# State-space stage: decay from sums broadcast by DMA, block output made transposed

## The chip, the cores and the metric

The kernel runs on one core of a Trainium2 chip. The metric is the time of one execution on the device, in microseconds (us). The engines are named as in the profile: PE is TensorE's matmul, PEld its weight load, DVE is VectorE, ACT is ScalarE, POOL is GpSimd, SP is SyncE, which here only issues DMAs.

## The reference, cut to what matters

The program is a two-layer decoder over 16 sequences of 128 tokens and width 256. Each layer has an attention-like part, a cross attention and a feed-forward part; the change lies in the attention-like part of the second layer, a state-space block with 8 heads of width 64, a state of 128 and chunks of 64. In the reference it reads (cut):

```python
xn = _rmsnorm(x, norm_w)
zxbcdt = xn @ in_proj_w                      # z: 512, xBC: 768, dt: 8
dt = jax.nn.softplus(zxbcdt[..., -NHEADS:] + dt_bias)
conv = conv_b + sum((xpad[:, k:k + T, :] * conv_w[:, k] for k in range(D_CONV)))
xBC = jax.nn.silu(conv)                      # xs: 512, Bm: 128, Cm: 128
y = _ssd(xs * dt[..., None], dt * A, Bm, Cm) # y_t = sum over s <= t of (C_t . B_s) exp(cs_t - cs_s) dt_s xs_s
y = y + xs * D[None, None, :, None]
y = _rmsnorm(y * jax.nn.silu(z), ssm_norm_w)
y = y @ out_proj_w
```

Here `cs` is the running sum of `dt * A` along the tokens, per head. The result `y` is then scored, the best tokens are gathered into a memory of 50 slots, and attention over that memory follows. A sequence has 128 tokens, so the kernel computes the whole recurrence of a sequence as one lower triangular 128x128 product per head.

## The kernel before, in words

A token block is one sequence: 128 tokens on the 128 partitions, 16 blocks in all. `K.x[b]` holds the residual of block b in SBUF during the whole kernel. The stages follow each other: mixture of experts (stage 0), cross attention and feed-forward of layer 0 (stage 1), the state-space block and its memory (stage 3), cross attention of layer 1 (stage 4), mixture of experts of layer 1 (stage 5). Everything is in float32 in the stage at hand.

The functions of `ssm` do the following. `normed(g)` normalizes a group of four blocks and turns it, so that `xnT[g]` has features on partitions and 512 tokens along the row. `convolved(g, c)` makes 128 channels of the convolution for the 512 tokens of group g: two products, one ACT operation, three DVE taps, a Tanh, and a finishing DVE operation (L1296); the result `cT[g]` is transposed too, channels on partitions. `steps()` makes `dt` and `da = dt * A` for all blocks at once, tokens on partitions.

Then for each block n. `decay(n)` makes the decay matrix `mT` of the 8 heads, source token on partitions and target token along the row: POOL writes `run`, the upper triangle times `da`; two products with the strictly lower triangle turn it into differences of running sums (`ps_seg`); ACT takes the exponential. `inner(n)` makes the product of B and C (`ps_s`), masks it on DVE (`bc`), and POOL multiplies `mT` by it; PE turns the four 128-channel pieces of `cT` (`px`), and DVE makes `xd` (times `dt`) and `yr` (times `D`) from them. `gate(n)` makes z with tokens on partitions, and its SiLU (`sz`). `outer(n)` multiplies, for each head, `mT` by `xd` into `py`, with tokens on partitions; DVE adds `yr`, POOL multiplies by `sz`, ACT squares with a sum along the row, POOL makes the reciprocal root `yrs`. `turned(n)` transposes the gated value by four PE transposes and an ACT copy, `projected(n)` applies the output projection, ACT scales by `yrs`, and DVE adds to the residual. `kept(n)` turns the result into `m.yT`; `remembered(g)`, `ranked(g)` and `counted(g)` do scores and ranks for each group of four blocks.

The order of work is set in two ways. PE's instructions stand in the order of the program text (`manual_schedule` for PE alone). Those of the other engines and of SP are put in order by a scheduler when the program is built, which takes what it expects to be ready first; buffers of a tag (two for `work` and `small` unless said otherwise) are given out as their last users finish. Each engine then executes its list in order. [...]

The main loop at L1519 is software-pipelined by hand: its pass n holds `decay` and `inner` of block n + 1, `turned` and `projected` of block n - 1, `outer` of block n, `kept` of block n - 2 and `gate` of block n + 1, and in passes 0 to 2, 4 to 6 and 8 to 10 two of the six convolutions of the next group. Before the loop, `others` makes products of the keys and values of stage 4 (`kv_banks`), which fill PE's waits, and writes them to DRAM over SP's queue.

## Time and profile before

| | |
|---|---|
| median of 3 runs | 1417.05 us (1410.79 to 1418.67) |
| the profiled execution | 1416.04 us, span of its instructions 1414.3 us |
| PE busy | 1263.7 us (89%) |
| DVE busy | 831.3 us (59%) |
| ACT busy | 648.3 us (46%) |
| POOL busy | 472.1 us (33%) |
| mean granted TensorE clock | 0.960 |
| chain that ended last | PE 61%, DVE 23%, ACT 6%, POOL 4%, issue 3%, DMA 2% |

The profile is of one execution. A row of a timeline gives the start in us from the beginning of the span, the time from the first to the last end of the instructions merged in it, the engine, the line, the operation, what it writes and reads, and how many there are (x4). In brackets stands how long the engine had been idle before, and what released it. A float32 product appears as two records. Successive PE records overlap in the trace, since a product's end is modelled with its way through the array; the cost of a step is therefore taken from its start to the start of the next one. A row of groups gives the count, the busy time in us, the mean duration of one in ns, and the idle time before them.

### The profile page before, as it was taken

What the parts mean: (1) busy time and instruction counts of PE and PEld (TensorE: products, weight loads), DVE (VectorE), ACT (ScalarE), POOL (GpSimd) and SP (SyncE); (2) the same over time, 40 slices, a digit from 0 to 9 for tenths busy, and PEclk for the clock granted to TensorE, in tenths of its full rate; (3) what the DMA queues carried; (4) which work ended last, traced back from release to release, by engine and by line L of the source; (5) the groups of instructions that cost most, each with busy time, mean ns of one, the idle gap of its engine ahead of it and who ended that gap; (6) DMA issues with size and microseconds to landing.
All of it is one profiled execution on the core that took longest, in us unless ns stands there. A gap on an engine that the chain in (4) does not pass through costs nothing.

```text
span 1414.3 us, 19193 instructions
## 1 busy us (share of the span) xinstructions
PE 1263.7 (89%) x6771; PEld 857.3 (61%) x6771; DVE 831.3 (59%) x1745; ACT 648.3 (46%) x1701; POOL 472.1 (33%) x627
## 2 busy tenths in 40 slices
PE   3678888889979999988998999999889999999995
PEld 1455444666654666656745688877777555666553
DVE  7789978989957766766745456567433211211115
ACT  5779865778955544432222556655522111111110
POOL 4256547667851654451033223322202000000003
PEclk9799989989999999998899999999999999999998
DMA  9358334110011000000100122221005221232002
GB/s 314 126 179 285 116 82 82 16 39 31 32 46 67 9 0 1 1 1 0 60 1 1 45 91 75 67 69 46 1 9 186 68 97 60 88 104 92 20 8 74
DMA packets 60272, 95.08 MB, mean 67 GB/s; under 512 B 11248, under 2 KB 40912, under 8 KB 59920
## 3 DMA queue, kind: packets, MB, share of 16 engines
q1 hardware_dynamic: 58000, 88.31, 18.5%
q0 software_dynamic: 2176, 5.55, 2.1%
q8 instruction: 53, 0.87, 0.2%
q14 instruction: 43, 0.35, 0.1%
HBM read 73.35 MB, written 16.29 MB: 63 GB/s over the span
## 4 chain that ended last, share of the span: by engine, by line
PE 61%; DVE 23%; ACT 6%; POOL 4%; issue 3%; DMA 2%; SPq 0%; DVEq 0%; ACTq 0%; POOLq 0%
PE ps_y L2227 7%; PE ps_m L2216 7%; PE ps_g L2216 7%; PE ps_m L1772 4%; PE ps_m L1285 3%; ACT s L1874 2%; PE ps_t L1894 2%; PE ps_y L1411 2%; PE ps_m L1903 2%; PE ps_y L1391 2%; PE ps_m L1792 2%; PE ps_m L1379 1%; DVE s L915 1%; DVE m L1868 1%; DVE s L1864 1%
## 5 line engine op out<-in xcount | busy, mean ns | idle before, releaser
L2221 DVE TENSOR_TENSOR h<-h,ps_m 128x512 f32<-128x512 f32 x60 | 41.3, 688 | 228.3 <-PE ps_m L2216 228.3
L82 POOL TENSOR_SCALAR ln_t<-ln_mv 128x1 f32<-128x1 f32 (+1 forms) x84 | 16.3, 193 | 451.8 <-DVE ln_mv L90 308.6
L1874 ACT ACTIVATE s<-s,m 128x128 f32<-128x128 f32 x256 | 99.3, 390 | 69.1 <-DVE m L1868 69.1
L2220 ACT ACTIVATE h<-ps_g 128x512 f32<-128x512 f32 x60 | 35.8, 597 | 171.0 <-PE ps_g L2216 171.0
L2216 PE MATMUL ps_g<-xin,w 128*128 128x512 f32 x224 | 106.3, 592 | 0.0
L2216 PE MATMUL ps_m<-xin,w 128*128 128x512 f32 x224 | 105.3, 592 | 0.0
L2227 PE MATMUL ps_y<-w,h 128*128 128x256 f32 x448 | 97.8, 379 | 0.0
L2227 PEld LDWEIGHTS ps_y<-w,h 128*128 128x128 f32 x448 | 85.1, 190 | 14.6 <-issue 3.3
L1878 POOL TENSOR_TENSOR s<-s,t 128x1024 f32<-128x1024 f32 x32 | 60.7, 1897 | 87.8 <-DVE t L1877 87.8
L927 ACT ACTIVATE s<-s,m 128x128 f32<-128x128 f32 x256 | 83.3, 394 | 14.2 <-DVE m L922 14.2
L2216 PEld LDWEIGHTS ps_m<-xin,w 128*128 128x128 f32 x224 | 42.5, 190 | 51.4 <-issue 50.2
L2216 PEld LDWEIGHTS ps_g<-xin,w 128*128 128x128 f32 x224 | 42.0, 190 | 46.4 <-issue 45.0
L1772 PE MATMUL ps_m<-xT,half 128*128 128x256 f32 x256 | 61.3, 384 | 2.6 <-DVE qT L1777 1.9
L1864 DVE TENSOR_TENSOR s<-ps_s,hide 128x1024 f32<-128x1024 f32 x32 | 39.2, 1224 | 36.1 <-PE ps_s L1861 36.0
L1903 PE MATMUL ps_m<-half,oT 128*128 128x256 f32 x256 | 59.3, 385 | 0.0
L2228 ACT COPY y<-ps_y 128x256 f32<-128x256 f32 x30 | 11.2, 372 | 104.7 <-PE ps_y L2227 66.2
L1291 DVE SCALAR_TENSOR_TENSOR acc<-ps_m,l1a_conv_w,acc 128x508 f32<-128x508 f32 (+2 forms) x72 | 52.7, 737 | 8.6 <-ACT acc L1287 8.3
L1903 PEld LDWEIGHTS ps_m<-half,oT 128*128 128x128 f32 x256 | 47.4, 190 | 7.5
L1772 PEld LDWEIGHTS ps_m<-xT,half 128*128 128x128 f32 x256 | 46.5, 190 | 9.0 <-DVE qT L1777 2.3
L83 POOL TENSOR_TENSOR ln_rs<-ln_t,mhalf 128x1 f32<-128x1 f32 (+1 forms) x84 | 48.7, 580 | 7.0
L1874 ACT ACTIVATION_READ_ACCUMULATOR s<-s,m 128x1 f32 x256 | 48.2, 188 | 0.0
L1345 POOL TENSOR_TENSOR run<-upper,da 128x1024 f32<-128x1024 f32 x16 | 30.7, 1924 | 46.8 <-DVE da L1337 26.7
(509 smaller groups left out, 3121.0 us busy)
## 6 DMA issues: line engine op xcount, KB each, us to landing
w<-in_w_gate_dram SPq DMA_DIRECT2D x9, 1024.0 KB, 6.7
w<-in_l1f_gateT_dram SPq DMA_DIRECT2D x14, 512.0 KB, 4.5
w<-in_l1f_upT_dram SPq DMA_DIRECT2D x14, 512.0 KB, 6.1
w<-in_l1f_downT_dram SPq DMA_DIRECT2D x14, 512.0 KB, 5.1
k<-kv SPq DMA_DIRECT2D x20, 256.0 KB, 2.4
v<-kv SPq DMA_DIRECT2D x20, 256.0 KB, 2.0
ring<-k SPq DMA_DIRECT2D x10, 512.0 KB, 3.8
ring<-v SPq DMA_DIRECT2D x10, 512.0 KB, 3.3
```

The costliest lines, as they stand in the source:

```text
L83: return self.nc.gpsimd.tensor_tensor(out, t, self.mhalf[: out.shape[0], :n], ALU.pow)
L927: nc.scalar.activation(at, at, AF.Exp, bias=m[h][:, i:i + 1])
L1285: nc.tensor.matmul(pc, w.inp[:, k, at:at + P], xnT[g][:, k, :], start=(k == 0), stop=(k == KD - 1))
L1291: nc.vector.scalar_tensor_tensor(accv[:, :, j:], pcv[:, :, :P - j], w.conv[:, c, TAPS - 1 - j:TAPS - j], accv[:, :, j:], ALU.mult, ALU.add,)
L1772: nc.tensor.matmul(pq[:, j, :], wt[k][:, at], src[:, k, :], start=(k == 0), stop=(k == KD - 1))
L1864: nc.vector.tensor_tensor(half(b, j), pss.rearrange("p r c k -> p (r c) k"), hide.unsqueeze(1).to_broadcast([P, 8, P]), ALU.add,)
L1874: nc.scalar.activation(at, at, AF.Exp, bias=m[j][:, i:i + 1], accum_out=t[j][:, i:i + 1])
L1878: nc.gpsimd.tensor_tensor(half(b, j), half(b, j), t[j].unsqueeze(2).to_broadcast([P, 8, P]), ALU.mult)
L1903: nc.tensor.matmul(py[b], oT[b][:, c, :], w.o[c // 4][:, c % 4, :], start=(c == 0), stop=(c == NC - 1))
L2216: nc.tensor.matmul(ps[:, j, :], m[k][:, c * P:(c + 1) * P], self.r.xin[:, k, e, cols], start=(k == 0), stop=(k == KD - 1),)
L2221: nc.vector.tensor_tensor(h, h, pu, ALU.mult)
L2227: nc.tensor.matmul(pd, rows(c), w.down[c // 4][:, c % 4, :], start=(c == 0), stop=(c == FI // P - 1))
```

## The change

The decay is made another way. `sums()` makes the running sums of `da` once for all blocks, in two forms: tokens on partitions (`cs`), and tokens along the row with one row per block and head, which goes to DRAM (`cs_dram`). `spread(n)` reads the 8 rows of block n back by a DMA that repeats them on all 128 partitions (`csb`, 512 KB). `decay(n)` is then a subtraction on POOL, and a Relu and an Exp on ACT over 128x1024; it has no product.

The block's output is made transposed. In `outer(n)` the product of a head has `xd` as weights (64 columns) and `mT` as the moving operand (128 columns); two heads write the two halves of the partitions of a bank. `gate` makes z transposed for two blocks at a time, half of its channels per call. The skip with `D` becomes part of the four DVE operations that read `py`, with `D` loaded in a form that has channels on partitions. `turned(n)` is gone. The sum of squares is now across partitions: ACT squares, POOL adds the four pieces in two operations, and in `scaled(n)` a product with one column of ones gives the sum; DVE and POOL make the reciprocal root. `projected(n)` keeps only its products.

In the order of work, `steps()` comes before convolution 4 of group 0, `sums()` and two `spread` after it; `gate(0)` and `gate(1)` come before the loop, and `gate(n + 2)` is in pass n. The bank tag `ps_seg` gives way to `ps_o`. `normed` takes its scratch from the tag `acc`.

```diff
-    w.dtb, w.a, w.d = (K.rows(pool, n, SH) for n in ("l1a_dt_bias", "l1a_A_log", "l1a_D"))
+    w.dtb, w.a = (K.rows(pool, n, SH) for n in ("l1a_dt_bias", "l1a_A_log"))
+    w.d = K.new(pool, [P, DI // P], F32, "l1a_D")
+    for j in range(2):
+        K.nc.sync.dma_start(
+            w.d[SP * j:SP * j + SP, :], K.ins["l1a_D"].rearrange("(c j) -> j c", j=2)[j].partition_broadcast(SP),
+        )
...
-                junk = K.new(work, [P, DI], F32, "sz")
+                junk = K.new(work, [P, DI], F32, "acc")
...
+        cs = K.new(grp, W, F32, "cs", bufs=1)
+        cs_dram = K.new(dram, [NB, SH * P], F32, "cs_dram")
+        csb = {}
+
+        def sums():
+            pc = K.new(ps, [P, 2, P], F32, "ps_m", bufs=3)
+            daf = da.rearrange("p n h -> p (n h)")
+            nc.tensor.matmul(pc[:, 0, :], daf, K.upper, start=True, stop=True)
+            nc.tensor.matmul(pc[:, 1, :], K.upper, daf, start=True, stop=True)
+            rows = K.new(work, [P, 512], F32, "acc")
+            nc.vector.tensor_copy(rows[:, :P], pc[:, 0, :])
+            nc.sync.dma_start(cs_dram.rearrange("n (h t) -> (n h) t", t=P), rows[:, :P])
+            nc.vector.tensor_copy(cs.rearrange("p n h -> p (n h)"), pc[:, 1, :])
+
+        def spread(n):
+            csb[n] = K.new(work, [P, SH, P], F32, "csb")
+            nc.sync.dma_start(csb[n].rearrange("p h t -> p (h t)"), cs_dram[n].partition_broadcast(P))
...
         def decay(n):
-            run = K.new(work, [P, SH, P], F32, "run")
+            st[n].mT = K.new(work, [P, SH, P], F32, "mT")
             nc.gpsimd.tensor_tensor(
-                run, K.upper.unsqueeze(1).to_broadcast([P, SH, P]),
-                da[:, n, :].unsqueeze(2).to_broadcast([P, SH, P]), ALU.mult,
+                st[n].mT, cs[:, n, :].unsqueeze(2).to_broadcast([P, SH, P]), csb[n], ALU.subtract,
             )
-            st[n].mT = K.new(work, [P, SH, P], F32, "mT")
-            for j in range(2):
-                half = slice(4 * j, 4 * j + 4)
-                pseg = K.new(ps, [P, 512], F32, "ps_seg")
-                nc.tensor.matmul(
-                    pseg, K.lower, run[:, half, :].rearrange("p h t -> p (h t)"), start=True, stop=True,
-                )
-                nc.scalar.activation(st[n].mT[:, half, :].rearrange("p h t -> p (h t)"), pseg, AF.Exp)
+            nc.scalar.activation(st[n].mT, st[n].mT, AF.Relu)
+            nc.scalar.activation(st[n].mT, st[n].mT, AF.Exp, scale=-1.0)
...
-            st[n].yr = K.new(work, [P, SH, SP], F32, "yr")
-            nc.vector.tensor_tensor(st[n].yr, pxh, w.d.unsqueeze(2).to_broadcast([P, SH, SP]), ALU.mult)
...
         def gate(n):
-            pz = K.new(ps, [P, DI], F32, "ps_m", bufs=3)
-            for k in range(KD):
-                nc.tensor.matmul(
-                    pz, xnT[n // 4][:, k, mine(n)], w.inp[:, k, :DI], start=(k == 0), stop=(k == KD - 1),
-                )
...
+            g, i = divmod(n, 2)
+            if i == 0:
+                sz[g] = K.new(work, [P, DI // P, 2 * P], F32, "sz")
+            pz = K.new(ps, [P, 2, 2 * P], F32, "ps_m", bufs=3)
+            at = slice(2 * g % 4 * P, 2 * g % 4 * P + 2 * P)
+            for j in range(2):
+                c = 2 * i + j
+                for k in range(KD):
+                    nc.tensor.matmul(
+                        pz[:, j, :], w.inp[:, k, c * P:(c + 1) * P], xnT[g // 2][:, k, at],
+                        start=(k == 0), stop=(k == KD - 1),
+                    )
+            to = sz[g][:, 2 * i:2 * i + 2, :]
+            nc.scalar.activation(to, pz, AF.Tanh)
+            nc.vector.scalar_tensor_tensor(to, to, 1.0, pz, ALU.add, ALU.mult)
...
         def outer(n):
             s = st[n]
-            py = K.new(ps, [P, SH, SP], F32, "ps_y")
-            for h in range(SH):
-                nc.tensor.matmul(py[:, h, :], s.mT[:, h, :], s.xd[:, h, :], start=True, stop=True)
-            nc.vector.tensor_tensor(s.yr, s.yr, py, ALU.add)
...
+            py = K.new(ps, [P, DI // P, P], F32, "ps_y")
+            for c in range(DI // P):
+                for j in range(2):
+                    nc.tensor.matmul(
+                        py[SP * j:SP * j + SP, c, :], s.xd[:, 2 * c + j, :], s.mT[:, 2 * c + j, :], start=True, stop=True,
+                    )
+            s.yf = K.new(work, [P, DI // P, P], F32, "yf")
+            for c in range(DI // P):
+                nc.vector.scalar_tensor_tensor(
+                    s.yf[:, c, :], cT[n // 4][:, c, mine(n)], w.d[:, c:c + 1], py[:, c, :], ALU.mult, ALU.add,
+                )
+            at = slice(n % 2 * P, n % 2 * P + P)
+            nc.gpsimd.tensor_tensor(s.yf, s.yf, sz[n // 2][:, :, at], ALU.mult)
+            s.sq = K.new(work, [P, DI // P, P], F32, "sq")
+            nc.scalar.activation(s.sq, s.yf, AF.Square)
+            for half in (2, 1):
+                nc.gpsimd.tensor_tensor(s.sq[:, :half, :], s.sq[:, :half, :], s.sq[:, half:2 * half, :], ALU.add)
...
+        def scaled(n):
+            s = st[n]
+            pn = K.new(ps, [P, 1], F32, "ps_s", bufs=1)
+            nc.tensor.matmul(pn, s.sq[:, 0, :], K.ones[:, :1], start=True, stop=True)
+            t = K.new(small, [P, 1], F32, "ys")
+            nc.vector.tensor_scalar(t, pn, 1.0 / DI, 1e-5, ALU.mult, ALU.add)
+            yrs = K.new(small, [P, 1], F32, "yrs")
+            nc.gpsimd.tensor_tensor(yrs, t, K.mhalf[:, :1], ALU.pow)
+            s.y = K.new(work, [P, D], F32, "y")
+            nc.scalar.mul(s.y, s.po, yrs)
+            nc.vector.scalar_tensor_tensor(x[n], x[n], 2.0, s.y, ALU.mult, ALU.add)
...
         for g in range(1, 4):
             others((1, 2, 2)[g - 1])
             normed(g)
-            convolved(0, 1 + g)
+            if g < 3:
+                convolved(0, 1 + g)
+        steps()
         others(1)
-        steps()
+        convolved(0, 4)
+        sums()
+        for n in range(2):
+            spread(n)
+        convolved(0, 5)
         others(2)
-        convolved(0, 5)
+        gate(0)
+        gate(1)
         others(2)
...
+            if n + 2 < NB:
+                spread(n + 2)
             if n + 1 < NB:
                 decay(n + 1)
-            if 0 < n <= NB:
-                turned(n - 1)
             if ahead:
                 convolved(g + 1, 2 * i)
+            elif n + 2 < NB:
+                gate(n + 2)
...
             if ahead:
                 convolved(g + 1, 2 * i + 1)
+            if 0 < n <= NB:
+                scaled(n - 1)
             if n < NB:
                 outer(n)
             if 1 < n <= NB + 1:
                 kept(n - 2)
-            if n + 1 < NB:
-                gate(n + 1)
+            if ahead and n + 2 < NB:
+                gate(n + 2)
```

## The prediction

> **What bounds the kernel now.** I read the page first (PE busy 89% of a span of 1414.3 us), then the busy time by stretches, then the timeline of one loop pass on PE, then the groups by form for prices. The program edited is the loop over 16 token blocks, 464 to 655 us.
>
> The busy time by stretches; columns: stretch, length, then PE, PEld, DVE, ACT, POOL busy (instructions), clock, DMA:
>
> ```profile
> 560.64:572.29 11.65, 11.65 (x54) 7.57 (x52) 7.22 (x13) 5.68 (x11) 5.88 (x5) 1.00 0.00 0
> 612.10:626.50 14.40, 10.15 (x46) 7.45 (x45) 8.06 (x19) 3.94 (x8) 7.23 (x6) 0.88 0.00 0
> 639.60:648.20 8.60, 8.53 (x45) 6.14 (x45) 3.56 (x7) 2.69 (x6) 3.32 (x2) 1.00 0.00 0
> 464.10:655.00 190.90, 178.93 (x843) 121.05 (x841) 127.56 (x232) 83.00 (x165) 94.47 (x74) 0.98 0.00 1
> ```
>
> PE fills 178.93 of 190.90 us. A pass with two convolutions (nine of them, "conv passes") is 11.65 us, all PE; one without is 8.60. The stretch at 612 is the exception: DVE is late with `counted(1)`.
>
> One conv pass on PE (start, us, what):
>
> ```profile
> 560.64 1.88 PE L1353 MATMUL ps_seg<-run,lower 128*128 128x512 f32 x4
> 562.35 0.60 PE L1403 MATMUL ps_m<-ident,yr 128*128 128x128 f32 x4
> 562.79 1.88 PE L1285 MATMUL ps_m<-xnT,l1a_in_proj 128*128 128x512 f32 x4
> 564.51 0.38 PE L1362 MATMUL ps_s<-cT 128*128 128x128 f32 x2
> 564.73 0.60 PE L1368 MATMUL ps_m<-ident,cT 128*128 128x128 f32 x4
> 565.17 1.89 PE L1411 MATMUL ps_y<-l1a_out_proj,yrT 128*128 128x256 f32 x8
> 566.89 1.88 PE L1285 MATMUL ps_m<-xnT,l1a_in_proj 128*128 128x512 f32 x4
> 568.61 1.89 PE L1391 MATMUL ps_y<-xd,mT 128*128 128x64 f32 x16
> 570.34 0.39 PE L1419 MATMUL ps_y<-ident,y 128*128 128x128 f32 x2
> 570.57 1.88 PE L1379 MATMUL ps_m<-l1a_in_proj,xnT 128*128 128x512 f32 x4
> ```
>
> Price each step from start to start: decay 1.71, turned 0.44, a convolution 1.72, `inner` 0.66, projected 1.72, outer 1.73, kept 0.23, gate 1.72.
>
> **Part by part, PE.** Removed per block: decay 1.71 and turned 0.44. `outer` now has weights of 64 columns and 128 moving columns, two heads in the two halves of the output. Stage 4 holds that very form, 32 records of it here:
>
> ```profile
> 900.45 1.97 PE L1894 MATMUL ps_t<-s,ring 128*64 128x128 f32 x32
> 902.35 1.16 PE L1861 MATMUL ps_s<-ring,qT 64*128 64x128 f32 x16
> ```
>
> 32 records in 1.90 us, so 16 take 0.95: the halves run together, 0.78 less than now. Bounds 0.95 and 1.73 (L1391); I take 0.95. Added: the one-column product in `scaled`, two records at 0.11 (a record's pitch in L1391), 0.22. `gate` has 8 records of 256 columns, as `projected`: 1.72, unchanged. Conv pass 11.65 - 1.71 - 0.44 - 0.78 + 0.22 = 8.94; without convolutions 5.50.
>
> **VectorE.** Pitches at 565 to 573: bc 0.20, xd 0.61, D product 0.60, adding py 0.59, x 0.33, sz 0.61, six taps 3.93, two finishes (L1296) 1.20: 8.07. The change drops 0.60 and 0.59, adds four 128x128 operations from PSUM (L1364: 0.20 pitch, 0.29 long; 1.0 for four) and one 128x1 (0.09, as L1444): 7.97. But see the beginning and length of these two:
>
> ```profile
> 574.25 1.90 POOL L1345 TENSOR_TENSOR run<-upper,da 128x1024 f32<-128x1024 f32 x1 [0.68 <-PE ps_seg L1353]
> 574.50 2.20 DVE L1296 SCALAR_TENSOR_TENSOR cT<-cT,acc 128x512 f32<-128x512 f32 x1 [0.69 <-ACT cT L1295]
> ```
>
> A finish, 0.69 by itself, took 2.20 when it began under a wide POOL operation: it waited for its end. It and the x update (two SBUF inputs) are three per conv pass. If they begin at random against POOL's five wide operations (below) in a 10 us pass, each waits the sum of squares 11.6 over 20, 0.58: 1.74 in all. The mean excess of L1296 now is 0.23 (0.917 against 0.685): 0.7. I take 1.74, as POOL is fuller: 9.7 us. [...]
>
> **GpSimd.** These forms price it:
>
> ```profile
> L1878 POOL TENSOR_TENSOR s<-s,t 128x1024 f32<-128x1024 f32 x32 | 60.7, 1897 | 87.8 <-DVE t L1877 87.8
> L935 POOL TENSOR_TENSOR sum<-s 128x1024 f32<-128x1024 f32 x16 | 38.1, 2384 | 2.5 <-ACT s L927 2.2
> L935 POOL TENSOR_TENSOR sum<-sum 128x256 f32<-128x256 f32 x16 | 11.9, 745 | 1.3
> ```
>
> The subtraction has L1878's operands, one full and one repeated along the row: 1.90 (at most 2.38, L935). Then the mask product 2.36 (L1365), gate product 1.27 (L1394), adds 0.745 and about 0.48 (halving less each time), power 0.55: 7.3 us, against 6.4 now. It idles 4 to 5 us a pass today; that cover is largely used up.
>
> **ScalarE.** Relu and Exp over 1024 columns about 1.06 each (0.63 at 512 in L1396, plus 0.43), 2.12 for 1.19; yrT's 0.58 and the accumulator read 0.19 go: 7.0 us for 6.8, hidden in a 10 us pass. Whether Relu reloads a table no run of it shows; a reload is 1.28 (L1334), 0 to 2.6 a pass. I take 0: Tanh, Exp, Square and copies alternate here without one.
>
> **Transfers.** SP issues nothing from 461 to 672. `spread` (512 KB) waits for the subtraction two blocks earlier to free its buffer and has nearly two passes: 3.8 us by ring<-k, 15.1 at worst (w_kv); hidden, 0. Uncovered, 3.8 once. Only the first lies near the path: sums at 453.8, copy and write 2.7, spread 3.8, subtraction 1.9, Relu and Exp 2.1, product 2.4 end by 469.3 at the latest input, and outer(0) is due at 470.6. Behind it in SP's queue stand only key/value writes that nobody awaits before 670. Loading D in two parts (3.3 us now) is 80 us early: 0; uncovered, 3.3.
>
> **New waits.** `steps` comes before convolution 4, so PE waits 1.8 us for xnT of group 3 and 2.7 for da; behind it queue convolution, k/v and gate products. `scaled`'s product waits for POOL's adds, and outer(n), kept and gate queue behind it; in a conv pass 7.8 us of PE work lies between, against a chain of about 5 (four DVE operations, gate product, square, adds) plus up to 2.4 of POOL's queue. Its bank is the one that `inner`'s first product uses, so the next `inner` waits until DVE has read it: nearly a pass later, 0; without that cover one DVE operation, 0.7. A gate's Tanh now writes a buffer that two blocks share, and waits for the gate product three blocks back; behind it on ACT stand Relu and Exp of the next block. In a conv pass that product is over; in the others it is the newest one, which `projected` awaits anyway: 0, at most 1.3. The squares in `normed` take their scratch from the convolutions' two buffers: 14 of 16 are done before the first convolution's result at 425.4, and the last group is not wanted before 442: 0; if each group had to wait for the convolutions before it, about 6 for each of three groups.
>
> **The sum**, against the profiled execution, 1416.04 us (span 1414.3 plus 1.7 around it), 1.0 under the median of 1417.05. A conv pass: DVE's 9.7 is above PE's 8.94; the pass at 639.6 runs 5% over its 8.2 of PE steps, so 10.15: 1.5 saved in each of eight, 12.0. Passes 5 and 9 carry `remembered` (4.4 of PE), PE bounds them: 0.7 more each, 1.4. Passes without convolutions: POOL's 7.3 and the 0.8 it waits for the square, 8.1. Pass 3 (12.3, with 2.1 of waiting and slow clock) 10.0, saved 2.3; pass 7, 0.5; 11 and 12 together 23.0 to 21.0 (`counted(1)`, 10.8 of DVE, stays), 2.0; pass 13, with `remembered`, 2.3; pass 14, 0.5; pass 15, where nothing covers turned and outer, 1.0: 8.6. Prologue and pass 0: decays 3.4, outer 0.8 and an old wait for a bank (1.4, at 459) go, 4.5 of new waits and the sums' 0.4 come, and pass 0 ends with one gate product (1.72) more done than now: 2.4. In all 12.0 + 1.4 + 8.6 + 2.4 = 24.4: **1392 us**. After the loop all starts as much earlier; nothing there is an absolute date, and the tail's square, adds and power replace turning and copy at par.
>
> The clock: after 2.1 us of PE idle, projected took 3.33 instead of 1.89 at 502. More PE idle could give four such windows on the path, 1.5 each: 0 to 6, taken 0, in the range. Best case, DVE waits 0.7 and POOL idles little: PE nears 8.94 everywhere, 16 us more: 1376.
>
> **Rivals.**
> - *Halves don't overlap*, outer stays 1.73: PE 9.7 beside DVE's 9.7; costs 3 to 6: 1396. Against it: L1894. 5%.
> - *VectorE is the new bound at once.* If each finish falls under a long POOL operation, 1.5 apiece and 0.5 for x, DVE needs 11.5: only the passes without convolutions and the prologue gain, 10: 1406. 14%.
> - *GpSimd in series, without slower passes*: it holds sub, waits 2.3 for Relu and Exp, multiplies, waits 0.8 and 0.5: 11 us a pass; conv passes gain 0.6, others lose 2: 1416. 9%.
> - *GpSimd in series behind a busy ScalarE: slower.* Relu and Exp also queue behind convolution work (0.78 and 0.62 pieces), the gate product behind DVE's taps: 6.3 of waits, 13.6 a pass. Nine conv passes lose 2 each, the others about 4 in all: 1438. It decides from 4.4 us of POOL waits a pass. For it: `POOL yr <- DVE yr` already waits 58.2 us in 16. Against it: today POOL's operations are ordered to run a block early wherever a buffer is free. 13%.
> - The forecast, 59%.
>
> Half a per cent (7 us) is about what a measurement can tell from none: below 1410 faster, 0.78; between, 0.09; above 1424 slower, 0.13. The range 1376 to 1417 leaves out the slow case and a few per cent below.
>
> **Signs.** Right: outer's 16 records in 0.95; a conv pass near 10 us; L1296's mean near 1.2; POOL near 7.3 a pass; no PE wait on csb. Wrong: conv passes near 9 (DVE was not the bound), POOL idle over 3 us a pass on ACT mT, or PE standing at the one-column product for POOL's adds.

## The result, and the profile after

The changed kernel takes 1432.99 us (median of 4 runs, 1428.9 to 1436.67) against 1417.86 us (4 runs, 1410.79 to 1419.69): ratio 1.0117 [1.0077, 1.0156], slower. The forecast was 1392.

The stage that the change touches runs from the first key/value product in it (PE, 414 us) to the first product of the memory after it (673 us before). Four starts bound its pieces; all are read from PE's timeline of one profiled execution each (the changed kernel's, 1428.9 us, is the fastest of its four):

| | before | after | after less before | forecast |
|---|---|---|---|---|
| first key/value product to outer(0) | 55.57 | 71.49 | +15.9 | -2.4 |
| outer(0) to outer(15) | 182.67 | 184.49 | +1.8 | -22 |
| whole stage | 258.77 | 275.89 | +17.1 | -24.4 |

So there are two questions: where 16 us ahead of the loop come from, and where the loop's gain went. Busy time by stretches of the changed kernel (stretch, length, then PE, PEld, DVE, ACT, POOL busy with their instructions, granted clock, DMA share, GB/s): two convolution passes, then the loop.

```profile
531.16:542.25 11.09, 9.51 (x52) 6.60 (x51) 10.18 (x17) 5.82 (x10) 7.58 (x7) 1.00 0.13 49
485.41:496.32 10.91, 9.33 (x49) 6.42 (x48) 9.84 (x17) 5.71 (x9) 6.90 (x6) 1.00 0.14 48
485.41:669.90 184.49, 148.04 (x773) 108.27 (x772) 136.11 (x267) 80.34 (x128) 107.96 (x88) 0.90 0.11 35
```

The same stretch of the kernel before, outer(0) to outer(15):

```profile
469.92:652.59 182.67, 170.99 (x808) 116.24 (x807) 122.66 (x223) 79.70 (x159) 88.94 (x72) 0.98 0.00 1
```

PE did lose work: 23.0 us of busy time. It stands idle 36.5 us instead of 11.7, which is 24.8 more. And its clock is 0.90 instead of 0.98, so part of the 148 us is work at half speed, at a granted clock of 0.50 (sized below). No engine is full over the loop: VectorE, the fullest after PE, is busy 74%.

The sizes of the new instructions came out nearly as forecast (groups of the changed kernel from 412 to 690 us; mean ns of one behind the comma):

```profile
L1383 POOL TENSOR_TENSOR mT<-mT,bc 128x1024 f32<-128x1024 f32 x16 | 37.9, 2366 | 22.8 <-DVE bc L1382 22.8
...
L1370 POOL TENSOR_TENSOR mT<-cs,csb 128x1024 f32<-128x1024 f32 x16 | 30.3, 1895 | 22.5 <-DVE acc L1297 19.5 <-PE ps_y L1415 1.8 <-DMA csb<-cs_dram 0.6
...
L1302 DVE SCALAR_TENSOR_TENSOR cT<-cT,acc 128x512 f32<-128x512 f32 x24 | 27.9, 1162 | 5.5 <-ACT cT L1301 5.5
...
L1424 POOL TENSOR_TENSOR yf<-yf,sz 128x512 f32<-128x512 f32 x16 | 21.8, 1363 | 36.1 <-DVE yf L1420 34.0 <-DVE key L1494 2.1
...
L1373 ACT ACTIVATE mT<-mT 128x1024 f32<-128x1024 f32 x16 | 16.9, 1056 | 18.3 <-POOL mT L1370 18.3
...
L1447 DVE SCALAR_TENSOR_TENSOR x<-x,y 128x256 f32<-128x256 f32 x16 | 16.1, 1007 | 8.5 <-ACT y L1446 8.5
```

The new waits of the loop, 485 to 670 us (engine and line, what it waited for, us in total, times, longest):

```profile
PE ps_o L1435 <- POOL yf L1424: 12.6, 10, 2.0
...
PE ps_m L1488 <- DVE acc L1484: 10.4, 2, 5.2
```

and the second of them in the kernel before, 470 to 653 us (there PE waits for the gate product only once, 4.3 us at `turned`):

```profile
PE ps_m L1455 <- DVE acc L1451: 4.0, 2, 2.0
```

Ten times PE stands at `projected` for the gate product, twice for 5.2 us in `ranked` for the diagonal that VectorE makes. One such pass of the changed kernel, in order of time (start, us, engine, line, operation; in brackets the idle time before it and its releaser):

```profile
531.16 1.09 PE L1415 MATMUL ps_y<-mT,xd 128*64 128x128 f32 x16
...
532.13 0.73 DVE L1297 SCALAR_TENSOR_TENSOR acc<-ps_m,l1a_conv_w,acc 128x508 f32<-128x508 f32 x1
...
532.59 1.89 POOL L1370 TENSOR_TENSOR mT<-cs,csb 128x1024 f32<-128x1024 f32 x1
...
533.16 1.60 DVE L1447 SCALAR_TENSOR_TENSOR x<-x,y 128x256 f32<-128x256 f32 x1 [0.29 <-ACT y L1446]
...
534.68 0.73 DVE L1297 SCALAR_TENSOR_TENSOR acc<-ps_m,l1a_conv_w,acc 128x504 f32<-128x504 f32 x1
535.34 0.33 DVE L1420 SCALAR_TENSOR_TENSOR yf<-cT,l1a_D,ps_y 128x128 f32<-128x128 f32 x1
535.48 0.58 ACT L1406 ACTIVATE sz<-ps_m 128x512 f32<-128x512 f32 x1
535.59 0.73 DVE L1297 SCALAR_TENSOR_TENSOR acc<-ps_m,l1a_conv_w,acc 128x500 f32<-128x500 f32 x1
...
536.24 0.85 DVE L1420 SCALAR_TENSOR_TENSOR yf<-cT,l1a_D,ps_y 128x128 f32<-128x128 f32 x3
...
537.17 1.27 POOL L1424 TENSOR_TENSOR yf<-yf,sz 128x512 f32<-128x512 f32 x1 [2.69 <-DVE yf L1420]
...
538.49 1.99 PE L1435 MATMUL ps_o<-l1a_out_proj,yf 128*128 128x256 f32 x8 [1.40 <-POOL yf L1424]
```

The outer products end at 532.2. VectorE's first operation on them begins 3.1 us later: its queue holds a convolution tap, then the x update, which began 0.6 us into GpSimd's subtraction and took 1.60 us (0.41 by itself), till the subtraction was over, then another tap. The four operations take till 537.1, the gate product till 538.4, and PE, which has only about 5 us of other work between `outer` and the next `projected`, has stood 1.40 us.

### The profile page after: what moved, and what is told of

It is laid out like the page before. It is cut to its first block, busy times and chain, and to the rows that moved or that the text cites. A ratio compares the mean times of both kernels' runs of the same rounds, so it can differ in the third digit from the quotient of the medians.

```text
span 1427.2 us, 19215 instructions
## 1 busy us (share of the span) xinstructions
PE 1242.2 (87%) x6743; PEld 850.1 (60%) x6743; DVE 846.8 (59%) x1795; ACT 649.5 (46%) x1669; POOL 489.1 (34%) x643
## 3 DMA queue, kind: packets, MB, share of 16 engines
q1 hardware_dynamic: 60848, 96.76, 20.4%
## 4 chain that ended last, share of the span: by engine, by line
PE 53%; DVE 27%; ACT 7%; POOL 6%; issue 4%; DMA 2%; SPq 0%; DVEq 0%; POOLq 0%; ACTq 0%
PE ps_y L2270 7%; PE ps_m L2259 7%; PE ps_g L2259 7%; PE ps_m L1815 4%; ACT s L1917 3%; PE ps_m L1946 2%; PE ps_t L1937 2%; DVE acc L1297 2%; PE ps_m L1291 2%; PE ps_m L1835 2%; DVE s L915 1%; PE ps_o L1435 1%; DVE m L1911 1%; DVE s L1907 1%; DVE m L922 1%
## 5 line engine op out<-in xcount | busy, mean ns | idle before, releaser
L2263 ACT ACTIVATE h<-ps_g 128x512 f32<-128x512 f32 x60 | 35.8, 597 | 171.0 <-PE ps_g L2259 171.0
L1435 PE MATMUL ps_o<-l1a_out_proj,yf 128*128 128x256 f32 x128 | 36.6, 436 | 16.5 <-POOL yf L1424 16.5
L1291 PE MATMUL ps_m<-xnT,l1a_in_proj 128*128 128x512 f32 x96 | 49.6, 644 | 0.4 <-DVE xnT L1282 0.4
```

The costliest lines, as they stand in the source:

```text
L1291: nc.tensor.matmul(pc, w.inp[:, k, at:at + P], xnT[g][:, k, :], start=(k == 0), stop=(k == KD - 1))
L1435: nc.tensor.matmul(s.po, s.yf[:, k, :], w.out[:, k, :], start=(k == 0), stop=(k == DI // P - 1))
```

## Experiments: the 16 us ahead of the loop

In the table, the pieces of each profiled execution as above. Whole times tell differences of half a per cent at best, since earlier stages put the start of the stage anywhere from 408.6 to 416.4 us. The first piece repeats better: in scratch_back and the five programs made from it that keep its order up to outer(0), it is 55.48 to 55.84 us. How far the loop of one program differs from execution to execution no run shows, as each program has one profile.

| label | ratio to before | first piece | loop | stage |
|---|---|---|---|---|
| before | 1 | 55.57 | 182.67 | 258.77 |
| after | 1.0117 [1.0077, 1.0156] | 71.49 | 184.49 | 275.89 |
| scratch_back | 1.0029 [1.0005, 1.0053] | 55.48 | 189.99 | 269.78 |
| scratch_alone | 1.0103 [1.0063, 1.0143] | 72.46 | 182.63 | 275.17 |
| decay_alone | 1.0008 [0.9984, 1.0033] | 58.36 | 182.65 | 261.56 |
| transposed_alone | 1.0054 [1.0033, 1.0075] | 56.87 | 183.67 | 263.44 |
| sub_on_scalar | 1.0017 [0.9995, 1.0039] | 55.49 | 182.53 | 258.87 |
| projected_later | 1.0008 [0.9988, 1.0028] | 55.78 | 183.91 | 259.98 |
| ranked_later | 1.0068 [1.0045, 1.0092] | 55.84 | 189.53 | 265.95 |
| all_three | 0.9979 [0.9945, 1.0012] | 55.52 | 177.31 | 253.29 |
| filled | 1.0118 [1.0067, 1.0169] | 55.72 | 192.75 | 275.42 |
| outer_first | 0.9993 [0.9971, 1.0016] | 54.43 | 180.02 | 258.48 |
| outer_first_sub | 0.9814 [0.9761, 0.9867] | 54.08 | 156.94 | 233.97 |
| outer_first_sub_ranked | 0.9851 [0.9797, 0.9906] | 54.08 | 155.03 | 231.29 |
| idle_subtraction | 0.9926 [0.9892, 0.9960] | 53.90 | 173.57 | 250.44 |
| three_mT | 1.0026 [1.0008, 1.0044] | 55.97 | 182.59 | 262.28 |

PE's timeline of the changed kernel shows a stand ahead of the loop that the kernel before does not have:

```profile
426.44 1.89 PE L1762 MATMUL ps_y<-ctxT,l1x_W_k 128*128 128x256 f32 x8
434.69 2.03 PE L1281 MATMUL ps_m<-ident,xn 128*128 128x128 f32 x8 [6.36 <-DVE xn L1276]
```

and ScalarE's timeline shows why: the squares of group 1 in `normed` begin when the Tanh of the second convolution is done, one group of four after another.

```profile
418.62 0.40 ACT L1271 ACTIVATE acc<-x 128x256 f32<-128x256 f32 x1
...
430.39 0.63 ACT L1301 ACTIVATE cT<-acc 128x512 f32<-128x512 f32 x1 [1.10 <-DVE acc L1297]
430.93 0.42 ACT L1271 ACTIVATE acc<-x 128x256 f32<-128x256 f32 x1
```

In the kernel before, 14 of 16 were done at 425.2, just ahead of the first convolution's ACT operation:

```profile
424.78 0.40 ACT L1265 ACTIVATE sz<-x 128x256 f32<-128x256 f32 x1
...
425.37 0.78 ACT L1287 ACTIVATE acc<-ps_m,l1a_conv_b,l1a_conv_w 128x512 f32<-128x512 f32 x1
```

**scratch_back.** The scratch of the squares gets its old tag back.

```diff
-                junk = K.new(work, [P, DI], F32, "acc")
+                junk = K.new(work, [P, DI], F32, "sz")
```

> The changed kernel with one line undone: the squares in normed take their scratch from the tag sz again, not from acc. Theory A (the squares had to wait for the convolutions to free acc): outer(0), at 485.4 us in the changed kernel and 469.9 before, comes back to 470 to 472, and the time is about 15 lower, 1418. Rival B (the new place of steps and the wait for the sums hold the prologue): outer(0) stays above 480 and the time above 1428.

1421.84 us (10 runs): most of the difference is gone. PE's timeline has no stand left at the transposes of groups 1 and 2:

```profile
425.09 0.60 PE L1281 MATMUL ps_m<-ident,xn 128*128 128x128 f32 x4
425.91 0.63 PE L1281 MATMUL ps_m<-ident,xn 128*128 128x128 f32 x4 [0.23 <-ACT kv L1532]
...
432.39 1.21 PE L1281 MATMUL ps_m<-ident,xn 128*128 128x128 f32 x8
```

**scratch_alone.** The kernel before with this one line changed.

```diff
-                junk = K.new(work, [P, DI], F32, "sz")
+                junk = K.new(work, [P, DI], F32, "acc")
```

> The kernel before with that one line of the change alone: the squares in normed take their scratch from acc. Theory A: outer(0) moves from 469.9 to about 482 to 485, and the time rises by 12 to 15, to about 1431. Rival B: within 3 us of before.

1432.99 us (4 runs): alone it costs the whole loss of the change, and the loop's 182.63 us are those of before. With both runs the cause is settled: the scratch shares its two buffers with the convolutions' sums, and a convolution holds one through its ACT operation, three taps and Tanh. (In scratch_back the loop is 5.5 us longer than in the changed kernel, so only 6.1 of the 16 us show in the stage. The two executions can account for that: the changed kernel's is 4.1 us below its median, that of scratch_back 2.1 above, and by the whole-time ratios the line is worth 0.0088, about 12.5 us. Whether the loop answers at all is not shown.)

## Experiments: where the loop's gain went

**decay_alone.** The kernel before with the new decay only: `sums`, `spread`, and

```diff
-                run, K.upper.unsqueeze(1).to_broadcast([P, SH, P]),
-                da[:, n, :].unsqueeze(2).to_broadcast([P, SH, P]), ALU.mult,
+                st[n].mT, cs[:, n, :].unsqueeze(2).to_broadcast([P, SH, P]), csb[n], ALU.subtract,
...
-                nc.tensor.matmul(
-                    pseg, K.lower, run[:, half, :].rearrange("p h t -> p (h t)"), start=True, stop=True,
-                )
-                nc.scalar.activation(st[n].mT[:, half, :].rearrange("p h t -> p (h t)"), pseg, AF.Exp)
+            nc.scalar.activation(st[n].mT, st[n].mT, AF.Relu)
+            nc.scalar.activation(st[n].mT, st[n].mT, AF.Exp, scale=-1.0)
```

> The kernel before with the new decay alone (sums, spread, subtraction, Relu and Exp), the block output still with tokens on partitions, the scratch and the order of steps as before. PE loses 1.71 us a pass. If PE bounds the loop as long as it is the fullest engine, the stretch from outer(0) to outer(15) falls from 182.7 to about 160 and the time to about 1395. If the longer way subtraction, Relu, Exp, product and the full GpSimd take PE's place at once, it falls by under 5 and the time stays above 1412.

1418.76 us (10 runs), no change, and the loop is 182.65 us to before's 182.67, although PE has lost 20.4 us of busy time in it. Where the decay products stood, PE now stands, at the four transposes of `turned` (here L1415; two of the waits of its loop):

```profile
POOL mT L1364 <- PE ps_y L1403: 36.7, 13, 6.1
...
PE ps_m L1415 <- POOL yr L1406: 19.7, 9, 6.8
```

The decay products had covered the way from the outer products over VectorE's addition and GpSimd's gate product to `turned`. Take them away and this way is what a pass takes. The new subtraction on GpSimd stands in it too: it waits for the outer products to free the decay tile (the first line), and in twelve passes the gate product follows it. But VectorE's addition ends only 0.2 to 0.5 us before it in nine of them, 1.2 in three, so it lengthens the way by no more than that. For the decay matrix, the long way of the second expectation, PE never waits.

**transposed_alone.** scratch_back with the old decay by products, their bank from `ps_o`.

```diff
-            nc.scalar.activation(st[n].mT, st[n].mT, AF.Relu)
-            nc.scalar.activation(st[n].mT, st[n].mT, AF.Exp, scale=-1.0)
...
+                pseg = K.new(ps, [P, 512], F32, "ps_o")
+                nc.tensor.matmul(
+                    pseg, K.lower, run[:, half, :].rearrange("p h t -> p (h t)"), start=True, stop=True,
+                )
+                nc.scalar.activation(st[n].mT[:, half, :].rearrange("p h t -> p (h t)"), pseg, AF.Exp)
```

> The changed kernel with the scratch back in sz and the old decay by products (its bank taken from ps_o): the transposed output alone. PE loses 0.44 + 0.78 - 0.22 = 1.0 us a pass. If PE bounds the loop, the stretch from outer(0) to outer(15) falls from 182.7 to about 168 and the time to about 1402. If the chain output, gate product, square, adds and one-column product (all before the next output on PE) is what holds the changed loop, it stays at 180 or more and the time at 1415 or more.

1422.19 us (10 runs). PE's busy time in the loop falls by 11.4 us (171.0 to 159.6), and the loop is 183.67: the other half of the change gains nothing by itself either. This run is less clean, since PE waits 6.5 us for the bank that the decay products share here with the projection; beside that it waits 8.0 us at `projected` for the gate product, 7.8 at `ranked`, and only 0.3 at the one-column product that the expectation named.

The next three start from scratch_back and ask what makes a pass long: the way between the engines, GpSimd's subtraction, or the stand at the ranking.

**sub_on_scalar.** The subtraction leaves GpSimd and becomes the bias of Relu.

```diff
-            nc.gpsimd.tensor_tensor(
-                st[n].mT, cs[:, n, :].unsqueeze(2).to_broadcast([P, SH, P]), csb[n], ALU.subtract,
-            )
-            nc.scalar.activation(st[n].mT, st[n].mT, AF.Relu)
+            for h in range(SH):
+                nc.scalar.activation(st[n].mT[:, h, :], csb[n][:, h, :], AF.Relu, bias=cs[:, n, h:h + 1], scale=-1.0)
```

> scratch_back (the changed kernel with the squares' scratch given back its own buffers) with the subtraction of the sums taken from GpSimd and put into ScalarE's Relu: per head a Relu of 128x128 with the head's own sum as its bias and scale -1, eight small operations in place of one of 1.06 us. GpSimd loses 1.90 us a pass, 15 of its 108 us become 80 in the loop; ScalarE gains about 1 us a pass (80 to 96 of 190). Theory lock and queue (VectorE's results for the gate are late since VectorE is slowed beside long GpSimd operations and GpSimd takes the subtraction ahead of the gate product): L1302's mean falls from 1.16 to near 1.0 and L1447's from 1.0 to near 0.6, the waits of TensorE for the gate product (14.8 us) halve, loop 190 to about 181, time near 1412. Rival (the stalls come from the order of VectorE's and TensorE's own work, not from GpSimd): waits unchanged, loop 188 to 192, time 1420 to 1424. Rival (ScalarE becomes late): waits for Exp ahead of the mask product, 1425 to 1430.

1418.45 us (10 runs). VectorE's finish (L1302) falls from 1236 to 860 ns and the x update from 1083 to 532 (466 to 656 us of both kernels): they had been held by the subtraction. The loop gains 7.5 us; the whole time's intervals overlap with those of scratch_back. PE's waits for the gate product stay: 12.4 us in 8.

**projected_later.** The projection behind the second convolution.

```diff
-            if 0 < n <= NB:
-                projected(n - 1)
             if ahead:
                 convolved(g + 1, 2 * i + 1)
             if 0 < n <= NB:
+                projected(n - 1)
                 scaled(n - 1)
```

> scratch_back with the out projection put behind the second convolution of a pass on TensorE instead of before it: 1.9 us more of TensorE's own work between the outer product and the projection that waits for its gated result. Theory chain (outer product, VectorE's four adds, GpSimd's gate product, projection is a chain with too little TensorE work beside it since the decay product and the transposes are gone): of 14.8 us of waits at the projection, 8 to 12 go in the nine convolution passes, the clock rises with them, time 1408 to 1413. Rival (VectorE's queue is the limit in these passes): the wait moves to the next product that needs a bank or a result, ones product, transposes or the convolution; time 1419 to 1424.

1414.06 us (10 runs). The waits at `projected` fall to 4.2 us in 4, as the chain theory has it, but 7.1 us in 6 at the ones product and 4.9 in 4 at the convolution appear, as the rival has it. The loop is 6 us shorter.

**ranked_later.** The rankings, and the counting behind two of them, one pass later.

```diff
-            if n > 2 and (n - 3) % 4 == 3:
-                ranked((n - 3) // 4)
-                for k in {6: (0,), 10: (1,), 18: (2, 3)}.get(n, ()):
+            if n in (7, 11, 15, 18):
+                ranked({7: 0, 11: 1, 15: 2, 18: 3}[n])
+                for k in {7: (0,), 11: (1,), 18: (2, 3)}.get(n, ()):
```

> scratch_back with the ranking of block scores one pass later, so that TensorE doesn't stand 5.2 us twice for the diagonal that VectorE makes from scores just computed, and doesn't run at half clock behind it. Theory clock and stall: 10.4 us of stalls and 5 to 8 us of half clock behind them, of which before had 2.0 us twice: 8 to 12 of them go, time 1410 to 1414. Rival (VectorE is late by its own queue, one pass later as well): the stall stays or moves, time 1419 to 1424.

1424.20 us (10 runs): a miss. The two waits of 5.2 us go, and 7.6 us at `inner`'s product for the finish and 4.8 at the ones product for `bc` come: VectorE is as late there. The loop is 189.5 us, 190.0 in scratch_back.

**all_three.** The three edits together.

```diff
+                nc.scalar.activation(st[n].mT[:, h, :], csb[n][:, h, :], AF.Relu, bias=cs[:, n, h:h + 1], scale=-1.0)
...
             if 0 < n <= NB:
+                projected(n - 1)
                 scaled(n - 1)
...
+            if n in (7, 11, 15, 18):
+                ranked({7: 0, 11: 1, 15: 2, 18: 3}[n])
```

> scratch_back with the three edits of this batch together. If each of the three takes away a cause of its own: 190 us of the loop become 160 to 165, time 1392 to 1400, which is below the kernel before. If they all take away the same waits: as the best of the three, 1408 to 1413. If VectorE's queue is the limit: 1415 to 1422.

1409.85 us (10 runs), in the range of the second expectation and not distinguishable from before. The loop is 12.7 us shorter than in scratch_back, while the three edits alone take off 7.5, 6.1 and 0.5, which is 14.0 together: by the loop they nearly add. So this run doesn't tell whether the causes are one or several.

**outer_first.** What keeps outer product and projection in one ring is PE's order: the projection of block n - 1 waits for its gate product, and `outer(n)` stands behind it in the queue. Here `outer(n)` goes ahead.

```diff
+            if n < NB:
+                outer(n)
+            if ahead:
+                convolved(g + 1, 2 * i + 1)
+            if 1 < n <= NB + 1:
+                kept(n - 2)
             if 0 < n <= NB:
                 projected(n - 1)
-            if ahead:
-                convolved(g + 1, 2 * i + 1)
-            if 0 < n <= NB:
                 scaled(n - 1)
-            if n < NB:
-                outer(n)
-            if 1 < n <= NB + 1:
-                kept(n - 2)
```

> scratch_back with another order of the tiles' steps on TensorE: a tile's outer products ahead of the projection of the tile before it, and the projection at the end of the pass, so that outer product, VectorE's adds, gate product and projection of one tile no longer stand between one outer product and the next. Theory chain (it is this ring of engines, not an engine's sum of work, that keeps a pass at 11 to 12 us while TensorE's own work shrank): the waits at the projection (14.8 us) nearly vanish, loop 190 to 172 to 178, time 1404 to 1410. Rival (VectorE beside GpSimd is full in the convolution passes): projected_later has already taken what there is, time 1412 to 1416, VectorE over 80% busy in them.

1414.57 us (10 runs): the waits at `projected` are gone, and the time is that of projected_later, as the rival said, though not by its reason: VectorE is busy 66% of the loop, and 65% of its eight intervals with convolutions. The waits point at ScalarE's queue (468 to 649 us):

```profile
ACT mT L1373 <- POOL mT L1370: 44.7, 14, 4.7
...
DVE acc L1297 <- ACT acc L1293: 17.2, 10, 2.5
```

Relu waits for the subtraction on GpSimd, and the first step of a convolution (L1293) stands behind it in ScalarE's queue, so that VectorE's taps come late (17.2 us; 2.6 in scratch_back) and with them the finish that PE waits for (5.6 us, once). That this queue holds the passes is read from the waits and not shown; idle_subtraction below leaves it a part at most.

**outer_first_sub.** outer_first and sub_on_scalar.

```diff
+                nc.scalar.activation(st[n].mT[:, h, :], csb[n][:, h, :], AF.Relu, bias=cs[:, n, h:h + 1], scale=-1.0)
...
+            if n < NB:
+                outer(n)
             if ahead:
                 convolved(g + 1, 2 * i + 1)
```

> outer_first with the subtraction in ScalarE's Relu as in sub_on_scalar. Theory: each edit takes a cause of its own (ring; GpSimd's long operation beside VectorE), so 3 to 5 us below outer_first, 1400 to 1406. Rival: with the ring opened, the subtraction is beside other work and costs nothing, same as outer_first within 2 us.

1390.26 us (4 runs, 1388.6 to 1391.45), ratio 0.9814 [0.9761, 0.9867]: far more than the 3 to 5 us expected over outer_first, and faster than both kernels. Each edit alone takes 7 to 10 us off scratch_back's loop, both together 33 (by the ratios 2 and 5 us, and 30). The loop:

```profile
466.73:623.67 156.94, 138.10 (x766) 100.06 (x766) 120.40 (x260) 100.53 (x227) 79.81 (x72) 0.95 0.14 46
```

PE is busy 88% of it again, at a clock of 0.95. VectorE's wait for L1293 is 2.0 us instead of 17.2; the waits at `ranked` are 0.8 us without a change there. The finish and the x update are no shorter than in outer_first (876 and 785 ns; 831 and 781 there), so in this order their being held is not what was gained.

**outer_first_sub_ranked.** The same with the rankings later.

```diff
+            if n in (7, 11, 15, 18):
+                ranked({7: 0, 11: 1, 15: 2, 18: 3}[n])
```

> outer_first_sub with the ranking one pass later. Theory: the two 5.2 us stands of TensorE at the ranking's diagonal and the half clock behind them are now the largest waits left, and with VectorE less late they go: 1392 to 1399. Rival (as in ranked_later alone): the wait only moves, same as outer_first_sub within 2 us.

1393.85 us (4 runs, 1390.37 to 1397.17): the rival; no difference that can be told. There was no stand at the ranking left to take.

**idle_subtraction.** Why is the subtraction so dear? outer_first_sub with the same work given back to GpSimd, into a scratch that nothing reads.

```diff
+            idle = K.new(work, [P, 512], F32, "kv").rearrange("p (h t) -> p h t", t=P)
+            for i in range(2):
+                at = slice(i * SH // 2, (i + 1) * SH // 2)
+                nc.gpsimd.tensor_tensor(
+                    idle, cs[:, n, at].unsqueeze(2).to_broadcast([P, SH // 2, P]), csb[n][:, at, :], ALU.subtract,
+                )
```

> outer_first_sub (1390.26) with GpSimd's subtraction put back as work without use: two halves of 128x512 of the same operands a tile, about 1.9 us together, written to a scratch that nothing reads; the decay itself still comes from ScalarE's Relu. Theory occupation (GpSimd's 1.9 us a pass in its in-order queue, and VectorE's two-input operations held up beside them, cost the 24 us between outer_first and outer_first_sub): most of it comes back, 1408 to 1415, with L1302's successor and the x update slower again. Rival (it was the step itself that cost: the subtraction waits for the outer products to free the buffer, and Relu, Exp and the mask product wait for it in series): the time stays near outer_first_sub, 1390 to 1396.

1403.48 us (6 runs), between the two. Its loop, and that of outer_first:

```profile
464.52:638.09 173.57, 144.17 (x767) 103.81 (x767) 124.65 (x260) 100.10 (x227) 115.78 (x105) 0.91 0.13 43
468.45:648.47 180.02, 145.52 (x766) 104.87 (x766) 119.46 (x260) 78.24 (x128) 105.77 (x86) 0.91 0.11 37
```

Of the 0.0179 by which the ratios of outer_first and outer_first_sub differ, 0.0112 come back, 63%; of the 23.1 us of the loops 16.6, 72%. So some two thirds of the price is GpSimd's time, though no result of it is awaited (the two halves take 1.10 us each, a little more than the 1.95 that they stand for, so this is rather too high). That the rest is the decay waiting for it in series is argued, not shown. ScalarE does not wait for this work, and VectorE waits only 4.2 us for L1293: ScalarE's queue has no more than that rest. Nor is it mainly VectorE held beside GpSimd: finish and x update take 1006 and 833 ns instead of 876 and 785, some 3 us in the loop. By what way GpSimd's time costs the other 13 or so stays open; that its later operations come later in its list is the obvious reading.

**three_mT.** outer_first with a third buffer for the decay tile, paid for by one buffer for the sums.

```diff
-            csb[n] = K.new(work, [P, SH, P], F32, "csb")
+            csb[n] = K.new(work, [P, SH, P], F32, "csb", bufs=1)
-            st[n].mT = K.new(work, [P, SH, P], F32, "mT")
+            st[n].mT = K.new(work, [P, SH, P], F32, "mT", bufs=3)
```

> outer_first (1414.57, the subtraction on GpSimd) with three buffers for the decay tile instead of two, and one instead of two for the broadcast sums so that it fits. Theory buffer (the subtraction's wait for the outer products two tiles back, 7.6 us in the loop, is what holds the decay chain): time falls to 1395 to 1402. Rival (GpSimd's time and its neighbours, not the buffer): within 3 us of outer_first, 1411 to 1418. Rival (one buffer for the sums makes the spread late): above 1420, with GpSimd waiting for the broadcast.

1418.71 us (10 runs). It gains nothing, but it doesn't settle the buffer: GpSimd now waits 3.8 us in the loop for the broadcast, where outer_first has no such wait, and still 7.2 for the outer products (7.6 in outer_first). What that second wait stands for stays open.

**filled.** The clock by itself. scratch_back with products without use on PE ahead of the ranking's product.

```diff
             prow = K.new(ps, W, F32, "ps_m", bufs=3)
+            for _ in range(9):
+                nc.tensor.matmul(
+                    prow.rearrange("p b t -> p (b t)"), K.ones, xnT[3][:, 0, :], start=True, stop=True,
+                )
```

> scratch_back with nine products of 128x512 on data that are there already, put on TensorE ahead of the ranking's product, into the bank that this product then overwrites: 4.2 us of work with no use, where TensorE stood 5.2 us at two of the four places and about 2 at the others. Theory clock (a wait of 1.4 us and more is followed by some 3.4 us at half clock): the gate products behind the two long stands fall from 2.90 and 3.55 us to 1.89, the others too, and the granted clock of these stretches goes from 0.66 and 0.69 to near 1; the time changes little, 1418 to 1424, as at the other two places the filling costs 2 us. Rival (the low clock has another reason than the stand, as the kind of product or the memory traffic): they stay at 2.9 to 3.5 us.

1429.87 us (7 runs): the filling was mis-sized. A float32 product of 128x512 is two records of 0.44 us, so nine take 7.9 us and not 4.2, and at the two other places they cover nothing. But the clock answers. PE in scratch_back:

```profile
606.95 2.05 PE L1488 MATMUL ps_m<-acc,ones 128*128 128x512 f32 x2 [5.20 <-DVE acc L1484]
...
609.07 3.55 PE L1401 MATMUL ps_m<-xnT,l1a_in_proj 128*128 128x256 f32 x8
```

and in filled, where PE never stands at this place:

```profile
599.47 7.89 PE L1489 MATMUL ps_m<-xnT,ones 128*128 128x512 f32 x18
607.19 1.02 PE L1492 MATMUL ps_m<-acc,ones 128*128 128x512 f32 x2
608.05 0.28 PE L1496 MATMUL ps_s<-score,ident 128*128 128x4 f32 x2
608.19 1.97 PE L1401 MATMUL ps_m<-xnT,l1a_in_proj 128*128 128x256 f32 x8
```

The same products go at full speed, and the granted clock is 1.00 from 605 to 615 us, where scratch_back has 0.69 from 606 to 616. Here the half clock came with the stand, not with the kind of product: the eight records took 3.55 us behind 5.20 us of stand and 1.97 without it. What the traces show of the 1.4 and 3.4 us in the theory stands in the last section.

## Why the prediction was wrong

The sizes of single steps held. Sixteen records of `outer` took 1.03 us (0.95 forecast), so two heads do run together; the one-column product about 0.2; Relu and Exp 1.06 and 1.05 without a table load of Relu's; GpSimd 7.2 us a pass (108.0 in 15; 7.3 forecast); L1302 1.16 us ("near 1.2"); ScalarE's loop 80.3 us to 79.7; GpSimd's waits for the broadcast 0.6 us in all. VectorE needed 9.8 and 10.2 us in the two convolution passes shown above and 10.9 in a third at full clock (from 584.56 us), 9.7 forecast; the x update was held 0.59 us on average (1007 ns against 415 by itself), the finish 0.48 (1162 against 685), where the sum had 0.58 for each.

**The step that failed ahead of the loop** is the term that took the squares' scratch at 0. The prediction saw that the scratch comes from the convolutions' two buffers and priced the uncovered case, "about 6 for each of three groups"; the trace has 6.4 us of PE stand for the first of them and 15.9 for the whole piece. It took 0 because in the kernel before 14 of 16 squares are done ahead of the first convolution's result. But that time belongs to a scratch with buffers of its own. With shared ones the squares of group 1 are placed behind the convolutions of group 0, whose buffers they need, and the earliness that was the cover is the first thing to go.

**The step that failed in the loop** is "A conv pass: DVE's 9.7 is above PE's 8.94 ... so 10.15", and the 1.5 saved in each of eight passes. It took the largest sum of one engine plus 5% for a pass. Convolution passes at full clock took 10.9, 11.1 and 11.8 us (from one `outer` to the next, each with one gate product). Two without a gate product, which the new order puts into the pass before, took 10.0 and 8.6; with its 1.72 they are 11.7 and 10.4. All eight gained 4.3 us, 0.8 when the two gate products that moved are counted, where 13.4 were forecast. What such a pass takes in the trace is the ring: `outer`, VectorE's four operations behind taps and x update, gate product, `projected`, next `outer`. The prediction did weigh a chain against PE work, but for `scaled`'s product (7.8 us of PE work between), and not for `projected`, which stands only about 5 us behind `outer` since `turned` and the decay products are gone; its signs named the one-column product, and there PE waited only 2.0 us for GpSimd's adds and 2.0 for the bank. decay_alone shows the missing entry: the removed products cost nothing before, because they lay in a wait. But the ring is one of two causes: outer_first, which opens it, takes 10 of the 33 us that it takes off together with the subtraction. The trace of before had the sign: the 58.2 us in which GpSimd's gate product waits for VectorE, which the prediction quoted for a rival only.

**The clock term**, 0 to 6, taken 0, was mis-sized. Nine stretches of products in the loop after run at half speed, two before (granted clock 0.50 for 37.6 us in all after, the stands in it included, and for 6.8 before); against the same groups at full speed they lose, from start to start, about 17 us after and 3.4 before. That is 14 us more, and the mean clock is 0.90 against 0.98. PE's loop adds up with it: some 37 us less of work at full speed, 14 more of slow clock, 24.8 more of standing idle, together the +1.8. So PE lost nearly the work that the prediction took from it (40.6 in 15 passes), and the idle time and the slow clock behind it took it all back.

**The passes without convolutions** were to gain 8.6 in all. The two intervals that hold `ranked` and `counted` lost 4.7 and 6.3 us (11.9 to 16.6 from outer(6) to outer(7), 11.9 to 18.2 from outer(10) to outer(11)), each with a stand of 5.2 us that was 2.0 before, and each with 1.7 of a gate product that came later in the kernel before; the intervals after them took 3.0 and 3.7 less, the first of them for want of that gate product in good part. All seven together lost 6.1 us. At the first stand VectorE works from 559.4 to 566.9 us with one gap of 0.26, and the diagonal comes behind all of it. In outer_first_sub these stands are 0.8 us together, so they belong to VectorE's lateness in this order and not to the ranking itself.

**The rivals.** The slower case had the right place, GpSimd in series behind a ScalarE that holds Relu and Exp, and its point of decision, 4.4 us of GpSimd's waits a pass, was passed: the waits of GpSimd in the loop (31.3 for the VectorE results, 20.6 for `bc`, 11.1 for the squares, 7.6 for the mean and some smaller) are about 5 us a pass. Its 13.6 us for a pass was too much, since the waits run beside other work: in the loop the time is nearer to the third rival's. The 1433 that came out are mostly the scratch, which no rival held. Without it the change stands at 1.0029 [1.0005, 1.0053].

The gain that was forecast was there to be had: in outer_first_sub the stage is 24.8 us shorter than before, and it took an order in which no block's outer products wait for another block's projection, and a subtraction that GpSimd no longer does. One credit of the sum has no cost beside it: a gate product more ahead of the loop counts as 1.72 gained, and its own time there is charged nowhere.

## What to carry to other kernels

A step that is removed from an engine gains only what it held up: look whether the next instruction on that engine would otherwise have waited, and how long the way through the other engines to it is. Where a pass goes round several engines in fixed order, sum the ring as well as each engine, and break the ring in the order before shortening its parts; of two causes side by side, taking one can show little where taking both shows much (7 and 10 us of the loop, and 33). And an idle date read from the trace of before is no cover for a scratch that the change itself moves into shared buffers.

## What the runs showed of the hardware that was not expected

In the changed kernel's loop the granted clock is 0.50 in nine stretches: seven of 3.41 us, and two of 6.83 us (from 566.45 and 617.65 us) that begin in the two stands of 5.2 us and hold 5.6 and 4.3 us of PE work. Eight of the nine begin within a wait of PE of 1.64 us or more, or up to 2.3 us behind its end; near the ninth, at 658.61 us, the only wait is one of 0.26 us. The products in such a stretch lose 1.5 to 1.8 us against the same products at full speed (2.3 and 2.9 behind the two stands of 5.2 us), so that a wait of 1.64 to 2.03 us cost 1.8 to 2.1 times its length. But waits of 1.64, 1.84 and 1.96 us in the same loop (ahead of 604.68, 667.26 and 527.40) had no such stretch behind them. Eight records of 128x256 took 3.50 us instead of 1.89 behind a wait of 1.39 in scratch_back; behind waits of 1.40 (in the fence above), 1.45 and 1.94 they took 1.99. What decides between the two no run shows.

```profile
574.42 3.50 PE L1435 MATMUL ps_o<-l1a_out_proj,yf 128*128 128x256 f32 x8 [1.39 <-POOL yf L1424]
...
633.24 1.99 PE L1435 MATMUL ps_o<-l1a_out_proj,yf 128*128 128x256 f32 x8 [1.94 <-POOL yf L1424]
```

Useless products in place of a stand of 5.20 us kept the clock at 1.00 (filled, 605 to 615 us).

An x update of 0.41 us took 1.60 (the pass above), and a finish of 0.69 took 2.16 (at 543.72), when begun under GpSimd's subtraction; each ended 0.3 to 0.5 us after it. With the subtraction on ScalarE the means of the two fell by 0.55 and 0.38 us from scratch_back to sub_on_scalar, though not from outer_first to outer_first_sub (831 and 781 ns there, 876 and 785 here). The prediction had taken this from one finish of the kernel before (2.20 us at 574.50).
